# Three stores of a prologue moved to ScalarE's queue, a batch's keys asked for later, the attention pools opened one slot earlier

## Chip, core and metric

One NeuronCore of one Trainium2 chip runs the whole kernel in one launch. The metric is the device time of one execution in microseconds. All data are float32.

## The reference, cut

Four residual layers on x of 64 batches x 32 rows x 512 columns:

```python
x = x + einsum('bct,bcd->bdt', x, L0_weights[cond])            # 32x32 mix of the rows of a batch
x = x + x @ base_weight.T + base_bias + (x @ A[ids].T) @ B[ids].T   # linear layer with a rank 16 adapter
x = x + attention(x)                                           # below
x = x + einsum('bct,bcd->bdt', x, L3_weights[cond])
# attention: q, k, v = x @ Wq.T, x @ Wk.T, x @ Wv.T   (32 query heads, 8 key heads, D = 128)
#   q, k: RMS norm over D, weight, rotary turn by cache_seqlens + row
#   keys, values: 512 rows gathered by pages of 32 from a cache, then the batch's own 32 rows
#   scores masked where the cache row is not below cache_seqlens; softmax; @ values; @ Wo.T
```

## The kernel before, in words

The 2048 rows are 16 tiles of 128 rows (`NT`), four batches to a tile. Attention runs in two halves of the key heads (`NG` = 2), so there are 32 steps of one tile and one half, 128 units of one batch each, and four slots to a unit, one for each key head: slots 0 to 511. Projections are made for two tiles at a time (a *pair*) one pair ahead of the attention that uses them. The slots from -42 to -1 are a prologue: the first two layers (class `First`, tile by tile, two slots apart), the turning of the cache's keys into `kT_dram` (class `Turn`) and the projections of pair 0.

The order of the work is written out by hand. `at(slot, where, do, ...)` puts a call into a plan; `slot(i)` runs the places of slot i in a fixed order: fetch, pool, scores of the slot, values and turns of older slots, then out, pe, take, late, power, turn, dve, keep, act, store. Every engine executes its own instructions in that order and waits for what each needs. A semaphore wait ahead of an instruction holds up everything behind it on the same engine. DMAs started by SP, POOL and ScalarE stand in those engines' streams in the same way.

What the change touches lies between slots -9 and 4:

- Tile 15, the last of `First`, has its turned rows copied out of PSUM by ScalarE (`keep_out`, L497, tile `x_b`) in slot -6, its two sums made by VectorE (`sums`, L507 to L511, tiles `x_12` and `x_34`) in slot -5. `store` (L524) sends the rows to `xT_dram` in slot -5, and `store_sums` (L528) the sums to `xS_dram` in slot -4. For the last three tiles `queue()` gives POOL's queue, for the others SP's.
- In slot -2 the pool `first`, which holds all of the prologue's tiles, is closed, and the pools `pages`, `v`, `attn` and `ps_o` are opened; their tiles may take its memory. A new tile there waits until the old tiles have been read for the last time, by DMAs too.
- In slot -2 POOL also makes the first unit's mask `pen` (`mask`, L819) and starts the gathers of its values (`fetch_values`, L105, tile `v_sb`), two in each of slots -2 and -1. Between them stand the `power` calls of the norms (L725 and L727, tiles `ss` and `rstd`), which turn sums of squares that ScalarE made (L720) into factors that VectorE applies (L732, then L739, L751, L761: the rotary turn).
- In slot 0, `scores` runs two matmuls (L848, L851) into `s_ps`; VectorE adds `pen` and finds the row's top (L856); ScalarE takes the exponentials (L867). There is one `s_ps`, so the next slot's scores wait for L856.
- SP fetches a unit's 16 key pages (`Unit.__init__`, L804, tile `kT`, two buffers): unit 0 in slot -8, unit 1 in slot -1, each later unit in the first slot of the unit before it. SP also loads the next pair's operands: `x_a`, `x_12`, `x_34`, `x_b` (L590) in slots -10, -7, -1, 0 and the rotary factors `rot_k` (L595) in slot 1. L706 stores new values (`vn`) from slot 1 on.

## Time and profile before

| | |
|---|---|
| median of 3 runs | 2436.03 us (2434.91 to 2437.69) |
| the profiled execution | 2439.1 us |
| its span, first to last instruction | 2437.3 us |
| granted TensorE clock | 0.999 |
| TensorE busy | 2401.4 us, 99% of the span |
| VectorE, ScalarE, POOL busy | 68%, 57%, 51% |
| DMA | 452.09 MB, mean 185 GB/s |
| TensorE's share of the chain that ended last | 94% |

Times in the profile are microseconds from the start of the span. Engines are PE (TensorE), PEld (its weight loads), DVE (VectorE), ACT (ScalarE), POOL (GpSimd) and SP; a q behind the name is the queue's own instructions, such as starting a DMA. A timeline row reads: start, length, engine, line and operation, output<-input, count, and in brackets the idle time ahead of it with what ended it. A row of waits reads: who waited, for whom, us in total, times, the longest. A row by stretch reads: stretch, length, then busy time and instructions of PE, PEld, DVE, ACT, POOL, the granted clock, the DMA engines' busy share and GB/s.

### The profile page before, as it was taken

Reading aid. Unit: us, or ns where it says so; the run is one execution under the profiler, and the core shown is the slowest. Engines: PE = TensorE matmul, PEld = TensorE weight load, DVE = VectorE, ACT = ScalarE, POOL = GpSimd, SP = SyncE. Lnnn points to the kernel's source line nnn. Section 1 sums busy time; section 2 is a strip of 40 time slices with the busy share of each in tenths; the row PEclk is TensorE's granted clock in tenths of the full one; section 3 lists DMA queues with packets and bytes.
Section 4 is the critical chain, followed back from the end, with each engine's and each line's share of the span. In section 5 each row is a group of like instructions: output and inputs, shape, how many; then the busy total and the mean of one; then the engine's idle time right before and its main releaser. Section 6 shows DMA issues by size and latency. Waiting matters only on the chain.

```text
span 2437.3 us, 47128 instructions
## 1 busy us (share of the span) xinstructions
PE 2401.4 (99%) x13794; PEld 1865.4 (77%) x13794; DVE 1647.1 (68%) x3554; ACT 1400.6 (57%) x4006; POOL 1234.5 (51%) x1271
## 2 busy tenths in 40 slices
PE   8999999999999999999999999999999999999999
PEld 5657777777777777777777777777777788888887
DVE  6557777777777777787777777777787756333222
ACT  2346777777777777777777777767677763000000
POOL 3336665566565657665665666565556663000000
PEclk9999999999999999999999999999999999999999
DMA  8876667676766677766566666666667874333221
GB/s 275 257 235 188 199 188 204 186 206 184 203 184 203 190 214 241 231 188 194 175 184 176 191 176 184 181 187 182 179 184 225 254 244 144 107 119 122 87 91 58
DMA packets 461199, 452.09 MB, mean 185 GB/s; under 512 B 67744, under 2 KB 384032, under 8 KB 457360
## 3 DMA queue, kind: packets, MB, share of 16 engines
q1 hardware_dynamic: 405104, 269.05, 36.7%
q0 software_dynamic: 55024, 179.25, 25.0%
q8 instruction: 111, 1.82, 0.3%
q14 instruction: 144, 1.18, 0.2%
q10 hardware_dynamic: 816, 0.79, 0.1%
HBM read 380.73 MB, written 76.55 MB: 188 GB/s over the span
## 4 chain that ended last, share of the span: by engine, by line
PE 94%; DMA 2%; DVE 1%; SPq 1%; ACT 1%; issue 1%; POOL 0%; ACTq 0%; DVEq 0%; POOLq 0%
PE proj_ps L664 23%; PE o_ps L900 18%; PE out_ps L1370 15%; PE s_ps L848 10%; PE pT_ps L890 9%; PE s_ps L851 9%; PE head_ps L766 3%; PE l_ps L481 2%; PE o_ps L913 1%; DMA kT<-kT 1%; SPq L804 1%; PE s_ps L883 1%; PE x1T_ps L450 1%; PE proj_ps L1179 1%; DMA o<-oT 1%
## 5 line engine op out<-in xcount | busy, mean ns | idle before, releaser
L105 POOL DMA_INDIRECT v_sb<-v,v_rows x512 | 543.3, 1061 | 361.6 <-PE o_ps L900 248.3
L900 PE MATMUL o_ps<-pT,v_sb 128*128 128x128 f32 x4096 | 624.9, 275 | 3.3 <-DVE pT L892 3.1
L900 PEld LDWEIGHTS o_ps<-pT,v_sb 128*128 128x128 f32 x4096 | 578.0, 191 | 32.2 <-DVE pT L892 5.4
L867 ACT ACTIVATE sm<-sm,top 128x544 f32<-128x544 f32 x512 | 380.8, 744 | 332.8 <-DVE top L856 241.5
L856 DVE CUSTOM_DVE_ANT_0 sm<-s_ps,pen 128x544 f32<-128x544 f32 x512 | 368.9, 721 | 115.4 <-PE s_ps L851 100.0
L873 ACT ACTIVATE sm<-sm,share 128x512 f32<-128x512 f32 x512 | 369.8, 722 | 108.6 <-DVE share L872 71.0
L892 DVE COPY pT<-pT_ps 128x512 f32<-128x512 f32 x512 | 352.9, 689 | 65.5 <-PE pT_ps L890 16.4
L848 PE MATMUL s_ps<-kT,qT 128*128 128x288 f32 x1024 | 334.7, 409 | 4.5 <-DVE top L856 2.7
L890 PE MATMUL pT_ps<-ident,sm 128*128 128x128 f32 x2048 | 310.0, 274 | 4.8 <-ACT qT L778 3.4
L676 DVE TENSOR_TENSOR raw<-proj_ps,raw 128x512 f32<-128x512 f32 x332 | 224.1, 687 | 131.2 <-PE proj_ps L664 118.8
L851 PE MATMUL s_ps<-kT,qT 128*128 128x256 f32 x1024 | 304.7, 379 | 1.3 <-issue 0.7
L848 PEld LDWEIGHTS s_ps<-kT,qT 128*128 128x128 f32 x1024 | 179.2, 190 | 152.4 <-issue 129.9
L819 POOL TENSOR_SCALAR pen<-key_f,seq_f 128x544 f32<-128x544 f32 x128 | 283.7, 2216 | 13.5 <-DMA kT<-kT 2.2
L890 PEld LDWEIGHTS pT_ps<-ident,sm 128*128 128x128 f32 x2048 | 239.3, 142 | 8.7 <-ACT qT L778 4.6
L720 ACT ACTIVATE sq<-raw 128x128 f32<-128x128 f32 x640 | 198.4, 310 | 73.2 <-DVE raw L676 54.6
L851 PEld LDWEIGHTS s_ps<-kT,qT 128*128 128x128 f32 x1024 | 194.4, 190 | 55.7 <-ACT sm L867 1.1
L105 POOL DMA_INDIRECT mix_rows<-in_w,cond_rows x32 | 37.1, 1160 | 343.7 <-DVE mix_diag L170 299.8
L872 DVE RECIPROCAL share<-total 128x1 f32<-128x1 f32 x512 | 83.8, 164 | 179.1 <-ACT sm L867 150.7
L725 POOL TENSOR_SCALAR ss<-ss 128x4 f32<-128x4 f32 x160 | 38.4, 240 | 311.0 <-ACT sq L720 305.1
L1424 ACT COPY p<-out_ps 128x256 f32<-128x256 f32 x7 | 2.6, 372 | 333.1 <-PE out_ps L1370 333.1
L664 PE MATMUL proj_ps<-sum,x 128*128 128x512 f32 x380 | 188.0, 597 | 0.0
L727 POOL TENSOR_TENSOR rstd<-ss,minus_half 128x4 f32<-128x4 f32 x160 | 169.5, 1059 | 13.3
(178 smaller groups left out, 3572.4 us busy)
## 6 DMA issues: line engine op xcount, KB each, us to landing
kT<-kT SPq DMA_DIRECT2D x2048, 64.0 KB
o_in<-o SPq DMA_DIRECT2D x28, 1024.0 KB
o<-oT POOLq DMA_DIRECT2D x68, 256.0 KB
o<-oT SPq DMA_DIRECT2D x58, 256.0 KB
v<-in_kv_cache SPq DMA_DIRECT2D x32, 256.0 KB
kT<-page_rows SPq DMA_DIRECT2D x32, 256.0 KB
vn<-raw SPq DMA_DIRECT2D x32, 256.0 KB
v_sb<-v,v_rows POOLq DMA_INDIRECT x512
```

The source lines that it names most:

```text
L105: nc.gpsimd.indirect_dma_start(out=dst, out_offset=None, in_=table, in_offset=bass.IndirectOffsetOnAxis(ap=index, axis=0),)
L664: nc.tensor.matmul(self.ps, lhsT=self.pair.x[x][:, c if x == "b" else half.start + c, :], rhs=blocks(self.b)[w][:, c, :], start=(c == 0), ...
L819: nc.gpsimd.tensor_scalar(self.pen, key_f, seq_f[:, self.b : self.b + 1], BIG, ALU.is_ge, ALU.mult)
L848: nc.tensor.matmul(ps[:, first:HID], lhsT=q, rhs=self.kT[:, :n1, k, :], start=True, stop=True)
L851: nc.tensor.matmul(ps[:, HID : first + LA], lhsT=q, rhs=self.kT[:, n1:, k, :], start=True, stop=True)
L856: nc.vector.tensor_tensor_reduce(out=sm, in0=ps[:, first : first + LA], in1=self.pen, scale=1.0, scalar=3e38, op0=ALU.add, op1=ALU.min, ac ...
L867: nc.scalar.activation(sm, sm, AF.Exp, bias=top, scale=-1.0, accum_out=total)
L873: nc.scalar.activation(sm[:, :L], sm[:, :L], AF.Copy, scale=share)
L890: nc.tensor.transpose(ps[:, c, :], self.sm[k][:, c * P : (c + 1) * P], ident)
L892: nc.vector.tensor_copy(pT, ps)
L900: nc.tensor.matmul(o_of[self.s, k][:, self.j, :], lhsT=self.v[c][:, k * D : (k + 1) * D], rhs=self.pT[k][:, c, :], start=(self.j == 0 and ...
L1370: nc.tensor.matmul(ps[:, :HALF], lhsT=o[:, i, :], rhs=w[i // REP][:, i % REP, :], start=(i == 0), stop=(i == KG * REP - 1),)
```

## The change

The last tile's `store` moves from POOL in slot -5 to ScalarE in slot -6 (place keep); its `store_sums` from POOL in slot -4 to ScalarE in slot -5 (place turn). Its `store_x` stays on POOL. Unit 1's key pages are asked for in slot 1 instead of -1, so behind `x_34`, `x_b` and `rot_k`. The pool `first` is closed, the attention pools are opened, and the first mask and gathers are made in slot -3 (and two gathers in -2) instead of -2 (and -1).

```diff
-            def queue(self):
-                return nc.sync if self.t < NT - 3 else nc.gpsimd
+            def queue(self, last=nc.gpsimd):
+                return nc.sync if self.t < NT - 3 else nc.gpsimd if self.t < NT - 1 else last
...
             def store(self):
-                self.queue().dma_start(out=xT_dram[self.t], in_=self.x2T)
+                self.queue(nc.scalar).dma_start(out=xT_dram[self.t], in_=self.x2T)
             def store_sums(self):
                 for i in (0, 1):
-                    self.queue().dma_start(out=xS_dram[self.t // 2][:, i], in_=self.s[i])
+                    self.queue(nc.scalar).dma_start(out=xS_dram[self.t // 2][:, i], in_=self.s[i])
...
-            at(home + 4, "store", call, *f, "store")
+            at(*((home + 4, "store") if t < NT - 1 else (home + 3, "keep")), call, *f, "store")
             if t % 2:
                 at(home + 4, "power", call, *f, "sums")
-                at(home + 5, "store", call, *f, "store_sums")
+                where = (home + 5, "store") if t < NT - 1 else (home + 4, "turn")
+                at(*where, call, *f, "store_sums")
...
-            at(KG * (u - 1) if u > 1 else (ready, -1)[u], "fetch", make, unit_of, u, Unit, u)
-            at(KG * (u - 1) + 1 if u else -2, "pool", call, unit_of, u, "mask")
+            at(KG * (u - 1) if u > 1 else (ready, 1)[u], "fetch", make, unit_of, u, Unit, u)
+            at(KG * (u - 1) + 1 if u else -3, "pool", call, unit_of, u, "mask")
             for c in range(NC):
-                at(KG * u - 2 + c if u else -2 + c // 2, "pool", call, unit_of, u, "fetch_values")
+                at(KG * u - 2 + c if u else -3 + c // 2, "pool", call, unit_of, u, "fetch_values")
...
-                if i == -2:
+                if i == -3:
                     first.close()
```

## The prediction

> **What bounds the kernel now.** I read four things in this order: the page (busy shares and the 40 slices), the busy time by stretch, the list of waits between 165 and 190 us, and the timeline of each engine there. TensorE is busy for 99% of the span and holds 94% of the chain that ended last, so a change off TensorE counts only where TensorE stands still. By stretch, that is at one place early on:

> ```profile
> 160.00:170.00 10.00, 9.72 (x36) 4.99 (x34) 6.90 (x14) 4.21 (x14) 1.60 (x4) 1.00 0.63 198
> 170.00:180.00 10.00, 5.69 (x19) 2.78 (x18) 5.58 (x11) 6.15 (x21) 7.21 (x8) 1.00 0.58 179
> 180.00:190.00 10.00, 8.05 (x38) 5.14 (x37) 8.35 (x22) 6.07 (x15) 8.54 (x8) 1.00 0.81 236
> 190.00:200.00 10.00, 10.00 (x58) 7.68 (x57) 5.88 (x14) 5.91 (x16) 6.52 (x9) 1.00 0.72 206
> ```

> The first number after the length is TensorE's busy time. From 170 to 190 us it lacks 4.31 + 1.95 = 6.3 us; before and after it is full, and the granted clock is 1.00 throughout. This is where the attention loop starts (slot 0), and the change edits just this place. The waits name the chain:

> ```profile
> DVE sm L856 <- POOL pen L819: 2.9, 1, 2.9
> ...
> PE s_ps L848 <- DVE top L856: 2.7, 1, 2.7
> POOL pen L819 <- DMA kT<-kT: 2.2, 1, 2.2
> ...
> PEld o_ps L900 <- DMA v_sb<-v,v_rows: 0.3, 1, 0.3
> ```

> TensorE's second scores wait for the first softmax on VectorE, that waits for the mask `pen` on POOL, and that waits for a DMA. Which DMA is seen on POOL's own timeline and in its semaphore waits ahead of L819:

> ```profile
> 169.70 1.05 POOL L727 TENSOR_TENSOR rstd<-ss,minus_half 128x4 f32<-128x4 f32 x1
> 170.72 0.63 POOL L524 DMA_DIRECT2D xT<-x_b  x1
> 171.35 1.08 POOL L528 DMA_DIRECT2D xS<-x  x2
> 172.51 0.48 POOL L725 TENSOR_SCALAR ss<-ss 128x4 f32<-128x4 f32 x1
> 173.07 1.07 POOL L727 TENSOR_TENSOR rstd<-ss,minus_half 128x4 f32<-128x4 f32 x1
> 176.33 2.12 POOL L819 TENSOR_SCALAR pen<-key_f,seq_f 128x544 f32<-128x544 f32 x1 [2.19 <-DMA kT<-kT]
> 178.73 1.11 POOL L105 DMA_INDIRECT v_sb<-v,v_rows  x1 [0.28 <-DMA kT<-kT]
> 180.14 0.96 POOL L105 DMA_INDIRECT v_sb<-v,v_rows  x1 [0.30 <-issue]
> 181.18 0.58 POOL L725 TENSOR_SCALAR ss<-ss 128x4 f32<-128x4 f32 x1
> 181.84 1.04 POOL L727 TENSOR_TENSOR rstd<-ss,minus_half 128x4 f32<-128x4 f32 x1
> ```
> ```profile
> L819 POOLq EVENT_SEMAPHORE  x8: 43/43/2567, 173.0 to 176.2; - x8
> ```

> The long one of the eight waits (2.567 us) is the third, 173.2 to 175.77. In the trace's record of semaphore increments that is the moment at which the second `xS` store of the last tile lands (issued 171.90, so 3.84 us); the name "kT" in the row is only the last DMA that the view found. `pen` takes memory of the pool `first`, which that store still reads. From the landing to `pen` it is 0.56 us.

> **Part 1: the three stores go to ScalarE.** POOL loses 0.63 + 1.08 us of issuing. ScalarE copies `x_b` from 166.21 to 166.80, issues `xT` behind it, then has the head copy (L778, 0.58) and four squares, which end at 169.30 now, and then issues the two `xS`; the sums that they store are ready at 168.39 (L511, 167.97 + 0.42). Rows of a DMA issued by ScalarE and of the same stores from SP:

> ```profile
> L255 ACTq DMA_DIRECT2D page_rows<-in_kv_cache x3: 420/477/1169, 11.8 to 12.8; - x3
> ```
> ```profile
> 129.60 0.89 SPq L528 DMA_DIRECT2D xS<-x  x2
> 130.59 0.45 SPq L521 DMA_DIRECT2D x<-x_sb  x1
> ...
> 134.40 0.33 SPq L398 DMA_DIRECT2D x_sb<-in_x  x1
> ```

> At 0.45 us each, `xT` delays ScalarE by 0.2 (it had a pause of 0.32 there), the squares end near 169.5, and the `xS` are issued at 169.55 and 170.03 instead of 171.35 and 171.90. In the built program the DMAs of SP and ScalarE take eight completion semaphores in turn, and each waits for the one before it on its semaphore; so ScalarE must first see the 10th, 12th and 13th key page of batch 0 land. They do at 166.1, 167.2 and 168.7 in the record of increments, before each is wanted: cost nothing, with 0.7 us of cover at the least. The landing: the pair on SP above took 3.56 and 3.58 us in the increments' record, and the `x` store behind it 3.74; POOL's took 3.84. I take 3.5 (the DMA share is a little lower here without the key pages), bounds 3.0 and 4.6 (the store at 138.44, landed 143.06). So the second `xS` lands at 170.03 + 3.5 = 173.5 and `pen` could start at 173.5 + 0.56 = **174.1 (bounds 173.6 and 175.2)**, 2.2 us earlier than now. ScalarE's eight later squares, the kT copy (173.31), the `raw` copy (173.50) come 1.1 to 1.2 us later, so TensorE's block at 175.55 does too; it is covered by TensorE's pause until 179.27, which has 2.7 us.

> [...]

> **Part 2: the mask and the gathers at slot -3.** This is the part that decides, and it costs. In the built order of the changed kernel POOL has `rstd` (the one of 169.70), then `pen`, two gathers, and only then the pair L725/L727 that now runs at 172.51. VectorE's order is unchanged: its L732 that needs this `rstd` stands ahead of the first softmax.

> ```profile
> 174.17 0.69 DVE L732 TENSOR_TENSOR raw<-raw,rstd 128x512 f32<-128x512 f32 x1 [0.21 <-POOL rstd L727]
> 174.90 0.69 DVE L739 TENSOR_TENSOR rot_a<-raw,rot_q 128x512 f32<-128x512 f32 x1
> 178.48 0.72 DVE L856 CUSTOM_DVE_ANT_0 sm<-s_ps,pen 128x544 f32<-128x544 f32 x1 [2.89 <-POOL pen L819]
> ```
> ```profile
> 179.27 0.75 PE L848 MATMUL s_ps<-kT,qT 128*128 128x288 f32 x2 [2.70 <-DVE top L856]
> ```

> So the `rstd` now waits for the store's landing, the mask and two gathers. From the start of `pen` to the end of an `rstd` behind it today's rows give 182.88 - 176.33 = 6.55 us (with 0.24 instead of 0.58 for L725: 6.2); I take 6.4. `rstd` ends at 174.1 + 6.4 = 180.5. L732 follows at once, L739 0.73 later, the softmax 0.60 to 0.69 after that: 180.5 + 1.4 = **181.9 against 178.48, so +3.4 us** on VectorE, and TensorE's second scores move from 179.27 to 182.7. What follows to 185 us (L751, L761, head turn, pT) hangs on the softmax, one behind another, and moves with it.

> What comes back: the third and fourth gather, now at 183.08 and 184.46, go at about 180.8 and 182.2, so TensorE's wait for the fourth (0.3 us, last line of the waits) goes: **-0.3**. The third `rstd` ends near 184.9 and is wanted 3.4 us later than today's 183.30, at 186.7: hidden, with 1.8 us of cover.

> **Part 3: batch 1's keys behind the pair's operands.** SP now issues `x_34`, `x_b`, two `rot_k` first: `x_34` at about 168.8, `x_b` when TensorE's last matmul on the old one is through (170.4), then the sixteen pages from about 172.9, 10.8 us as now, to 183.7; landing by 186 (1.7 to 3.7 us a page today). Three of these pages wait for the semaphores of ScalarE's stores, free by 173.5. They are wanted by the fifth scores, 190.55 today and 193.6 then: 7 us of cover, nothing on the path. `x_34` and `x_b` are wanted at 196 us or later. The vn store behind them waits for VectorE at 184.60 as it does today. Price **0**; if it reached TensorE, the delay would show as a wait of L848 on kT.

> **The sum.** +3.4 - 0.3 = **+3.1 us**. From 190 us on TensorE has no pause of this kind (all its waits from 190 to 2050 us add to under 13 us), so nothing gives it back. The profiled execution of 2439.1 us (span 2437.3) would be 2442.2 and the span 2440.4; its time is 3.1 us above the median of 2436.03, so I carry the difference to the median: **2439.1**. Per us of landing the sum moves by one us: delta = start of `pen` - 171.0. The bounds 173.6 and 175.2 with 6.2 and 6.55 give +2.4 and +4.4. A measurement of this kernel tells about 0.2%, 4.9 us, from no change.

> **The rivals.**
> - *Slower by more (0.12).* ScalarE's queue is the new bound of the store: an issue of 1.17 us (the longest of the ACTq row) for each instead of 0.45 puts the second `xS` at 171.7, and a landing of 4.6 us puts `pen` at 176.9: delta +5.9, **2441.9**. It decides 0.2% from a `pen` start of 175.9 on. For it: the only three such issues in the trace have one of 1.17. Against: the DMA share is 0.58 at 170 to 180.
> - *The mask leads (0.07).* The softmax follows `pen` and not `rstd`: -2.2 us, **2433.8**. For it: the wait that the view names. Against: in-order VectorE has L732 in front.
> - *It does not do what it says (0.07).* If key pages released `pen`, as the row is named, it would start at 170.8 at once, `rstd` would end at 177.2 and the softmax start at 178.6: no change, **2436**. Against: the 2.567 us wait ends with `xS`.

> **How the numbers follow.** The forecast has 0.74. Its bounds with the spread of the three runs (about 1.4 us either way) are 2437.0 to 2441.8; reaching a little towards the third rival gives 2436.4 to 2441.8, and leaves out the second rival and part of the first. Slower by over 0.2%: the first rival and 0.02 of the forecast's tail, 0.14; faster by over 0.2% needs 4.9 us, which none of these gives, 0.02; the rest 0.84.

> **What would show it.** Right: `pen` at about 174, the L725/L727 pair behind two gathers ending near 180.5, L732 waiting for it, first L856 near 182, TensorE's pause ahead of the second L848 near 6 us. Wrong: L856 before 178.5, a pause on kT at the fifth scores, or a ScalarE issue over 1 us.

## The result, and the profile after

| | before | after | ratio |
|---|---|---|---|
| median, 10 runs each | 2436.16 us | 2441.32 us | 1.0022 (95%: 1.0012 to 1.0031) |
| profiled execution (span) | 2439.1 us (2437.3) | 2437.26 us (2435.5) | |

The changed kernel is slower by about 5 us, with an interval of 3 to 7.5. The two spans say the opposite, because the profiled execution of after is the fastest of its ten and that of before is among its slower ones. What differs between those two for that reason lies near 1980 us and is shown at the end of this section. So the stretch that the change edits has to be compared by itself.

By stretch (start and end, length, busy time and instructions of PE, PEld, DVE, ACT, POOL, granted clock, DMA share, GB/s), after:

```profile
170.00:180.00 10.00, 4.67 (x15) 2.16 (x14) 3.35 (x6) 5.46 (x20) 6.01 (x6) 1.00 0.66 193
180.00:190.00 10.00, 7.84 (x22) 5.14 (x23) 7.56 (x19) 4.86 (x11) 8.57 (x10) 0.66 0.56 165
```

TensorE lacks 5.33 + 2.16 = 7.5 us of work here, 1.2 more than before. The granted clock of 0.66 in the second line is new, so part of the busy time is the same work done at a lower speed. The waits from 165 to 195 us name the new chain:

```profile
DVE raw L732 <- POOL rstd L727: 6.4, 1, 6.4
PE s_ps L848 <- DVE top L856: 5.9, 1, 5.9
...
POOL pen L819 <- DMA rot_k<-trig_all: 3.2, 1, 3.2
```

VectorE's wait for `pen` (2.9 us before) is no longer there. A wait of L732 for `rstd` stands in its place, more than twice as long. ScalarE's queue shows the two `xS` stores, and POOL's timeline shows why `rstd` is late:

```profile
168.75 0.34 ACTq L528 DMA_DIRECT2D xS<-x  x1
...
169.19 0.39 ACTq L528 DMA_DIRECT2D xS<-x  x1
```
```profile
169.50 1.05 POOL L727 TENSOR_TENSOR rstd<-ss,minus_half 128x4 f32<-128x4 f32 x1
173.80 2.12 POOL L819 TENSOR_SCALAR pen<-key_f,seq_f 128x544 f32<-128x544 f32 x1 [3.25 <-DMA rot_k<-trig_all]
176.20 1.11 POOL L105 DMA_INDIRECT v_sb<-v,v_rows  x1 [0.28 <-DMA kT<-kT]
177.62 0.96 POOL L105 DMA_INDIRECT v_sb<-v,v_rows  x1 [0.30 <-issue]
178.65 0.23 POOL L725 TENSOR_SCALAR ss<-ss 128x4 f32<-128x4 f32 x1
178.97 1.05 POOL L727 TENSOR_TENSOR rstd<-ss,minus_half 128x4 f32<-128x4 f32 x1
180.21 1.50 POOL L105 DMA_INDIRECT v_sb<-v,v_rows  x1 [0.20 <-issue]
182.00 0.95 POOL L105 DMA_INDIRECT v_sb<-v,v_rows  x1 [0.30 <-issue]
```

`pen` starts 2.5 us earlier than before (173.80 against 176.33). The pair L725/L727, 1.28 us of work, now stands behind it and two gathers and ends at 180.02; before, it ended at 174.14. The name "rot_k" in the bracket is again only the last DMA that the view found. The semaphore of the second `xS`, issued at 169.19, is full at 173.17 in the record of increments, and `pen` follows 0.63 later. VectorE and TensorE then:

```profile
180.05 0.69 DVE L732 TENSOR_TENSOR raw<-raw,rstd 128x512 f32<-128x512 f32 x1 [6.40 <-POOL rstd L727]
180.77 0.69 DVE L739 TENSOR_TENSOR rot_a<-raw,rot_q 128x512 f32<-128x512 f32 x1
181.38 0.72 DVE L856 CUSTOM_DVE_ANT_0 sm<-s_ps,pen 128x544 f32<-128x544 f32 x1
...
184.48 0.72 DVE L856 CUSTOM_DVE_ANT_0 sm<-s_ps,pen 128x544 f32<-128x544 f32 x1
```
```profile
182.16 1.33 PE L848 MATMUL s_ps<-kT,qT 128*128 128x288 f32 x2 [5.87 <-DVE top L856]
```

The softmax follows L732 and L739 with no wait for `pen`, which had been done since 175.92. TensorE's pause is 5.87 us instead of 2.70. Its first matmul after the pause takes 1.33 us instead of 0.75, because its clock is halved, to 0.50 from 180.79 to 187.61:

```profile
180.00:182.00 2.00, 0.00 (x0) 0.00 (x0) 1.92 (x3) 0.00 (x0) 1.51 (x2) 0.70 0.78 221
182.00:184.00 2.00, 1.84 (x4) 1.47 (x5) 1.06 (x6) 1.63 (x4) 1.84 (x3) 0.50 0.78 231
184.00:186.00 2.00, 2.00 (x4) 0.77 (x4) 1.21 (x3) 0.91 (x3) 1.90 (x2) 0.50 0.50 144
```

Both traces hold the same 13794 matmuls in the same order, so each can be set against its twin. I call the difference lateness, and take its growth from 172 us (ahead of the pause) to 190 us, so that what happened earlier drops out. For after it is **+3.1 us**. By 1900 us it is 0.3 us lower and by 1950 us 1.0 lower, with no step over 0.7.

What turns the two spans round is late. Waits of TensorE from 1945 to 2010 us in before (after has no row of this kind there), then the stretch from 1980 to 2000 us of before and of after:

```profile
PE s_ps L848 <- DMA kT<-kT: 1.6, 1, 1.6
PE s_ps L851 <- DMA kT<-kT: 0.6, 1, 0.6
```
```profile
1980.00:2000.00 20.00, 17.21 (x97) 14.49 (x97) 13.34 (x28) 10.21 (x25) 11.20 (x8) 0.91 0.78 249
```
```profile
1980.00:2000.00 20.00, 18.16 (x114) 15.64 (x115) 13.91 (x28) 10.73 (x26) 10.28 (x9) 1.00 0.75 246
```

In before's profiled execution, key pages come late there and the clock drops. Between 1952 and 2035 us the nine other profiles of this case change their lateness against it by anything from -5.5 to +0.8 us. That is as much as the runs of one kernel scatter (some 4 us either way), so a profile's span can't be used for an effect of 3 us.

### The profile page after: what moved, and what is told of

Its sections match the earlier page's. It is cut to its first block, busy times and chain, and to the rows that moved or that the text cites. A ratio compares the mean times of both kernels' runs of the same rounds, so it can differ in the third digit from the quotient of the medians.

```text
span 2435.5 us, 47125 instructions
## 1 busy us (share of the span) xinstructions
PE 2401.8 (99%) x13794; PEld 1865.5 (77%) x13794; DVE 1650.0 (68%) x3554; ACT 1401.0 (58%) x4006; POOL 1235.3 (51%) x1268
## 3 DMA queue, kind: packets, MB, share of 16 engines
q8 instruction: 111, 1.82, 0.3%
## 4 chain that ended last, share of the span: by engine, by line
PE 95%; DVE 1%; issue 1%; DMA 1%; ACT 1%; POOL 1%; SPq 0%; DVEq 0%; ACTq 0%; POOLq 0%
PE proj_ps L664 23%; PE o_ps L900 18%; PE out_ps L1371 15%; PE s_ps L848 10%; PE pT_ps L890 9%; PE s_ps L851 9%; PE head_ps L766 3%; PE l_ps L481 3%; PE o_ps L913 1%; PE s_ps L883 1%; PE x1T_ps L450 1%; PE h_ps L465 1%; PE mix_ps L1389 1%; PE proj_ps L1180 1%; PE pageT_ps L273 0%
## 5 line engine op out<-in xcount | busy, mean ns | idle before, releaser
L105 POOL DMA_INDIRECT v_sb<-v,v_rows x512 | 545.6, 1066 | 360.4 <-PE o_ps L900 251.7
L900 PE MATMUL o_ps<-pT,v_sb 128*128 128x128 f32 x4096 | 623.9, 275 | 1.7 <-DVE pT L892 1.7
L900 PEld LDWEIGHTS o_ps<-pT,v_sb 128*128 128x128 f32 x4096 | 577.4, 191 | 29.9 <-DVE pT L892 3.0
L856 DVE CUSTOM_DVE_ANT_0 sm<-s_ps,pen 128x544 f32<-128x544 f32 x512 | 369.3, 721 | 110.3 <-PE s_ps L851 97.5
L848 PE MATMUL s_ps<-kT,qT 128*128 128x288 f32 x1024 | 335.4, 409 | 6.3 <-DVE top L856 6.1
L890 PE MATMUL pT_ps<-ident,sm 128*128 128x128 f32 x2048 | 309.6, 274 | 2.3 <-ACT qT L778 2.2
L848 PEld LDWEIGHTS s_ps<-kT,qT 128*128 128x128 f32 x1024 | 179.4, 191 | 154.0 <-issue 129.2
L819 POOL TENSOR_SCALAR pen<-key_f,seq_f 128x544 f32<-128x544 f32 x128 | 283.7, 2216 | 14.6 <-DMA rot_k<-trig_all 3.2
L890 PEld LDWEIGHTS pT_ps<-ident,sm 128*128 128x128 f32 x2048 | 239.0, 142 | 5.9 <-ACT qT L778 3.2
L105 POOL DMA_INDIRECT mix_rows<-in_w,cond_rows x32 | 36.4, 1136 | 345.1 <-DVE mix_diag L170 301.2
L725 POOL TENSOR_SCALAR ss<-ss 128x4 f32<-128x4 f32 x160 | 38.6, 241 | 309.3 <-ACT sq L720 304.1
L727 POOL TENSOR_TENSOR rstd<-ss,minus_half 128x4 f32<-128x4 f32 x160 | 170.1, 1063 | 13.4
```

The costliest lines, as they stand in the source:

```text
L105: nc.gpsimd.indirect_dma_start(out=dst, out_offset=None, in_=table, in_offset=bass.IndirectOffsetOnAxis(ap=index, axis=0),)
L819: nc.gpsimd.tensor_scalar(self.pen, key_f, seq_f[:, self.b : self.b + 1], BIG, ALU.is_ge, ALU.mult)
L848: nc.tensor.matmul(ps[:, first:HID], lhsT=q, rhs=self.kT[:, :n1, k, :], start=True, stop=True)
L856: nc.vector.tensor_tensor_reduce(out=sm, in0=ps[:, first : first + LA], in1=self.pen, scale=1.0, scalar=3e38, op0=ALU.add, op1=ALU.min, ac ...
L890: nc.tensor.transpose(ps[:, c, :], self.sm[k][:, c * P : (c + 1) * P], ident)
L900: nc.tensor.matmul(o_of[self.s, k][:, self.j, :], lhsT=self.v[c][:, k * D : (k + 1) * D], rhs=self.pT[k][:, c, :], start=(self.j == 0 and ...
```

## The experiments

Diffs are against after unless they say otherwise. Each time is a median of 11 runs beside 33 of the kernel before (after's row is the result above, 10 beside 10): before was 2437.56 us for the first four kernels and 2436.46 for the other four. The table gathers what the traces show at the start of attention: when the mask `pen` and the first softmax (L856) start, and how long TensorE pauses ahead of its second scores (PE pause). "Half clock" is the length of the record of the granted clock at 0.5 there. "Late" is the growth of lateness as defined above.

| kernel | median us | ratio (95%) | `pen` | first L856 | PE pause | half clock us | late us |
|---|---|---|---|---|---|---|---|
| before | | 1 | 176.33 | 178.48 | 2.70 | 0 | 0 |
| after | 2441.32 | 1.0022 (1.0012 to 1.0031) | 173.80 | 181.38 | 5.87 | 6.83 | +3.1 |
| e1_again | 2439.25 | 1.0008 (0.9999 to 1.0017) | 173.55 | 181.15 | 5.62 | 6.83 | +2.7 |
| e2_stores_keys | 2434.78 | 0.9985 (0.9976 to 0.9994) | 175.06 | 177.22 | 1.55 | 0 | -0.8 |
| e3_slot3_only | 2441.86 | 1.0023 (1.0013 to 1.0032) | 177.13 | 184.68 | 8.25 | 10.24 | +5.2 |
| e4_no_gather_ahead | 2439.23 | 1.0006 (0.9995 to 1.0017) | 174.73 | 179.65 | 4.50 | 3.41 | +1.5 |
| e5_behind_rstd | 2437.70 | 1.0007 (0.9998 to 1.0016) | 173.57 | 176.28 | 0.73 | 3.41 | +0.6 |
| e6_stores_only | 2436.92 | 1.0000 (0.9991 to 1.0009) | 175.44 | 178.09 | 1.44 | 0 | -0.5 |
| e7_keys_only | 2438.47 | 1.0010 (1.0001 to 1.0019) | 176.78 | 178.94 | 3.06 | 6.83 | +0.6 |
| e8_stores_keys_2 | 2433.17 | 0.9990 (0.9981 to 0.9999) | 174.42 | 177.05 | 0.81 | 0 | -2.2 |

### The changed kernel again (e1_again)

No edit: it shows how far one measurement of the same kernel stands from the next.

> The changed kernel once more. If the loss is all at the start of attention (the rstd behind the mask and two gathers), TensorE is 3 us late at 200 us, no more at the end apart from scatter, and the median is about +3.1 us. If something else in the rest of the span costs too, it is about +5 us and the lateness grows after 200 us. The first softmax (L856) starts near 181.4, TensorE's pause ahead of the second L848 is near 5.9 us and the granted clock halves behind it.

The start of attention repeats within 0.3 us (`pen` 173.55, first softmax 181.15, pause 5.62), but the ratio is 1.0008 instead of 1.0022. The two intervals just overlap. Their mean, 1.0015, is some +3.7 us. Whether after loses more than the 3 us seen at its start stays within this scatter.

### Without slot -3 (e2_stores_keys and e8_stores_keys_2)

```diff
-            at(KG * (u - 1) + 1 if u else -3, "pool", call, unit_of, u, "mask")
+            at(KG * (u - 1) + 1 if u else -2, "pool", call, unit_of, u, "mask")
-                at(KG * u - 2 + c if u else -3 + c // 2, "pool", call, unit_of, u, "fetch_values")
+                at(KG * u - 2 + c if u else -2 + c // 2, "pool", call, unit_of, u, "fetch_values")
-                if i == -3:
+                if i == -2:
                     first.close()
```

> The stores on ScalarE and the later keys stay; pools, mask and gathers go back to slot -2. Theory (the rstd behind the mask is the whole loss): the rstd is made ahead of the mask again, pen starts near 173.8, the first softmax 2.15 us later at 176.0, TensorE's pause is under 1 us: -2.4 us against the kernel before, 2433.8. Rival (the stores on ScalarE or the later keys cost by themselves): slower than before, +1 us or more.

> The kernel with the stores on ScalarE and the later keys, pools at slot -2, once more: its first profile had a landing that let pen start at 175.1 and a gain of 0.6 us at the start of attention, its median was 3.6 us below the kernel before. If the landing scatters, pen starts at another time here, between 173.5 and 175.5, and the first softmax 2.15 us behind it. Median -1 to -3.6 us.

Rows of POOL and PE in e2, then in e8:

```profile
175.06 2.12 POOL L819 TENSOR_SCALAR pen<-key_f,seq_f 128x544 f32<-128x544 f32 x1 [1.72 <-DMA rot_k<-trig_all]
```
```profile
178.00 0.75 PE L848 MATMUL s_ps<-kT,qT 128*128 128x288 f32 x2 [1.55 <-DVE top L856]
...
188.47 0.49 PE L900 MATMUL o_ps<-pT,v_sb 128*128 128x128 f32 x2 [0.45 <-DMA v_sb<-v,v_rows]
```
```profile
174.42 2.59 POOL L819 TENSOR_SCALAR pen<-key_f,seq_f 128x544 f32<-128x544 f32 x1 [0.51 <-DMA rot_k<-trig_all]
```
```profile
177.84 0.75 PE L848 MATMUL s_ps<-kT,qT 128*128 128x288 f32 x2 [0.81 <-DVE top L856]
```

With the pair L725/L727 ahead of the mask again, the earlier store does bring the softmax forward, and the pause shrinks from 2.70 to 1.55 and 0.81. This is the only version that beats both kernels, twice: by 0.15% and by 0.10%, with both intervals below 1. The loss of after is therefore in the slot -3 part, and the two other parts together gain. The medians' 2.4 to 3.7 us (by the ratios) are more than the 0.8 and 2.2 that the traces show at the start; the rest has no place that I could show. The gather's wait, which slot -3 removes, is back as 0.45 us in e2.

### Slot -3 alone (e3_slot3_only)

Against before:

```diff
-            at(KG * (u - 1) + 1 if u else -2, "pool", call, unit_of, u, "mask")
+            at(KG * (u - 1) + 1 if u else -3, "pool", call, unit_of, u, "mask")
-                at(KG * u - 2 + c if u else -2 + c // 2, "pool", call, unit_of, u, "fetch_values")
+                at(KG * u - 2 + c if u else -3 + c // 2, "pool", call, unit_of, u, "fetch_values")
-                if i == -2:
+                if i == -3:
                     first.close()
```

> Only pools, mask and gathers at slot -3; stores on POOL, keys as before. Theory: pen starts as before near 176.2, the rstd behind it ends 6.2 us later near 182.4, the first softmax starts near 183.8 against 178.5, pause near 8 us: +5 us, 2441. Rival (the mask leads, its slot costs nothing): no change, L856 near 178.4.

```profile
183.34 0.69 DVE L732 TENSOR_TENSOR raw<-raw,rstd 128x512 f32<-128x512 f32 x1 [8.74 <-POOL rstd L727]
```
```profile
185.46 1.32 PE L848 MATMUL s_ps<-kT,qT 128*128 128x288 f32 x2 [8.25 <-DVE top L856]
```

With the stores still on POOL, `pen` starts at 177.13 and everything behind it moves with it: `rstd` ends 6.2 us after the start of `pen`, as in after. 1.0023 of 2437.56 is +5.6 us, near the lateness of +5.2. At the start of attention slot -3 alone costs more than the whole change (+5.2 against +3.1 and +2.7; the ratios, 1.0023 against 1.0022 and 1.0008, don't part them as clearly). The stores on ScalarE, with the later keys, take part of it back by letting `pen` start earlier.

### Only the mask ahead (e4_no_gather_ahead)

```diff
-                at(KG * u - 2 + c if u else -3 + c // 2, "pool", call, unit_of, u, "fetch_values")
+                at(KG * u - 2 + c if u else -2 + c // 2, "pool", call, unit_of, u, "fetch_values")
```

> As the changed kernel, but the gathers back in their old slots, so that only the mask stands ahead of the rstd. Theory: pen near 173.8, the rstd ends 3.6 us later at 177.4, the first softmax starts near 178.8 and TensorE's pause is near 3.3 us, without a halved clock: +0.4 us. Rival (the wait for the store's landing is what costs, not what stands between mask and rstd): as the changed kernel, +3 us or more.

```profile
174.73 2.12 POOL L819 TENSOR_SCALAR pen<-key_f,seq_f 128x544 f32<-128x544 f32 x1 [4.52 <-DMA kT<-kT]
176.93 0.23 POOL L725 TENSOR_SCALAR ss<-ss 128x4 f32<-128x4 f32 x1
177.25 1.04 POOL L727 TENSOR_TENSOR rstd<-ss,minus_half 128x4 f32<-128x4 f32 x1
```
```profile
180.43 1.33 PE L848 MATMUL s_ps<-kT,qT 128*128 128x288 f32 x2 [4.50 <-DVE top L856]
```

The store landed later in this execution (5.24 us after its issue at 168.87), so `pen` is 0.9 later than in after. Mainly for that the expectation was missed: the pause is 4.50 us instead of about 3.3, and the clock is halved for 3.41. Measured from `pen`, `rstd` ends 3.56 us on instead of 6.22. The two gathers account for the difference of 2.66, and the lateness falls from +3.1 to +1.5. It is the queue between the mask and `rstd` that sets the cost, with one part for each instruction in it.

### The same place, behind `rstd` (e5_behind_rstd)

```diff
-            at(KG * (u - 1) + 1 if u else -3, "pool", call, unit_of, u, "mask")
+            at(KG * (u - 1) + 1 if u else -3, "pool" if u else "turn", call, unit_of, u, "mask")
-                at(KG * u - 2 + c if u else -3 + c // 2, "pool", call, unit_of, u, "fetch_values")
+                at(KG * u - 2 + c if u else -3 + c // 2, "turn" if u == 0 and c < 2 else "pool", call, unit_of, u, "fetch_values")
```

> The changed kernel with one difference: within slot -3 the mask and its two gathers stand behind the norm's pair L725/L727 instead of ahead of it; pools still open in slot -3. Theory (the place in POOL's order is the loss, not the slot): the rstd is made near 172 to 173, the first softmax starts 2.15 us after pen, 176 to 177.5 with pen at 173.8 to 175.2, and the median is 1 to 3 us below the kernel before. The third rstd stands behind all four gathers here, so up to 1 us of it may come back at the third softmax. Rival (opening the pools at slot -3 or the moved DMAs cost by themselves): +1 us or more.

```profile
176.28 0.72 DVE L856 CUSTOM_DVE_ANT_0 sm<-s_ps,pen 128x544 f32<-128x544 f32 x1 [0.90 <-DMA kT<-kT]
...
183.00 0.69 DVE L732 TENSOR_TENSOR raw<-raw,rstd 128x512 f32<-128x512 f32 x1 [1.82 <-POOL rstd L727]
```
```profile
184.34 3.43 PE L664 MATMUL proj_ps<-sum,x 128*128 128x512 f32 x4 [1.00 <-DVE raw L676]
```

The slot and the stores are those of after; only the order on POOL differs. The first softmax comes at 176.28, 5.1 us earlier than in after and 2.2 earlier than before, and the pause ahead of the second scores shrinks to 0.73. So the order, and not the earlier opening of the pools, costs after its time. Not all of the gain is kept. Four gathers now stand ahead of the third pair L725/L727, VectorE waits 1.82 us for that one, and TensorE pauses 1.00 us and then has its clock halved once: the four matmuls at 184.34 take 3.43 us, where after's at 188.51 take 1.88. The lateness ends at +0.6 and the ratio at 1.0007, so the expected 1 to 3 us below before are not seen.

### The stores alone (e6_stores_only)

The edits of e2, and:

```diff
-            at(KG * (u - 1) if u > 1 else (ready, 1)[u], "fetch", make, unit_of, u, Unit, u)
+            at(KG * (u - 1) if u > 1 else (ready, -1)[u], "fetch", make, unit_of, u, Unit, u)
```

> Only the three stores on ScalarE; keys asked for at slot -1 and pools at slot -2 as before. Theory: the second xS is issued near 169.2 instead of 171.9 and lands at 173 to 174.5 amid the key pages, pen starts 1 to 2.5 us earlier than before and the first softmax with it: -1 to -2.5 us. Rival (with the key pages around it, ScalarE's store lands no earlier than POOL's): no change.

```profile
170.61 1.37 ACTq L528 DMA_DIRECT2D xS<-x  x2
172.10 0.31 ACT L720 ACTIVATE sq<-raw 128x128 f32<-128x128 f32 x1 [2.52 <-DVE raw L732]
```
```profile
175.44 2.62 POOL L819 TENSOR_SCALAR pen<-key_f,seq_f 128x544 f32<-128x544 f32 x1
```

The `xS` stores are issued almost 2 us later than in after, and ScalarE does no work for 2.5 us around them (169.58 to 172.10). The bracket names VectorE; the semaphores name the cause. In the built program the DMAs of SP and ScalarE take eight completion semaphores in turn (100 to 107 in the traces of before and after; in after the two stores have 101 and 102, wait for them at 168.70 and 169.14 and go at 168.75 and 169.19), and with batch 1's keys asked for early, the turn of the two stores falls behind the load of `x_12` and a key page of batch 1. In the record of increments that load is full at 170.53 and the page at 171.58; the stores go at 170.61 and 171.65. ScalarE's squares behind the stores are late too, the pair L725/L727 follows them (L725 at 173.89, done at 175.35), and `pen` starts only when that pair is done. The second store, which landed at 174.72, would not have let it start sooner: the last of the waits ahead of `pen` ends at 175.30. The stores alone gain nothing: 1.0000.

### The keys alone (e7_keys_only)

Against before:

```diff
-            at(KG * (u - 1) if u > 1 else (ready, -1)[u], "fetch", make, unit_of, u, Unit, u)
+            at(KG * (u - 1) if u > 1 else (ready, 1)[u], "fetch", make, unit_of, u, Unit, u)
```

> Only the later request for batch 1's keys. Theory: POOL's stores land 0 to 0.7 us earlier with fewer transfers beside them, the fifth scores wait for no key page: 0 to -0.7 us. Rival (the pages come too late): a wait of L848 on kT at the fifth scores, +1 us or more.

```profile
176.78 2.12 POOL L819 TENSOR_SCALAR pen<-key_f,seq_f 128x544 f32<-128x544 f32 x1 [2.54 <-DMA kT<-kT]
```
```profile
179.73 1.33 PE L848 MATMUL s_ps<-kT,qT 128*128 128x288 f32 x2 [3.06 <-DVE top L856]
```

This was a miss: slower by 0.10% (0.01 to 0.19), where nothing or a small gain was expected. `pen` starts 0.45 us later than in before (POOL's second `xS` store took 4.19 us to land, against 3.84), the pause of 3.06 us brings 6.83 us of halved clock, and the lateness is +0.6. TensorE has no wait on kT at the fifth scores. The ratio's 2.4 us are 1.8 more than that. In this one profile the lateness grows further, to +2.0 by 1900 us, in steps of at most 0.7 us; other profiles show steps as large or larger there, up and down, so the cause of these 1.8 us is open. Together with e6 and e2 it shows that the two parts need each other: alone they give 1.0000 and 1.0010, together 0.9985 and 0.9990.

## Why the prediction was right

It said +3.1 us, and the lateness is +3.1 at the place it named; the median's +5.2 holds it within its interval, and the repeat gives about +2. In absolute time the median of 2441.32 us lies 2.2 above the forecast of 2439.1, near the upper end of the range (2441.8). The steps in its own order:

| step | forecast | after |
|---|---|---|
| second `xS` issued on ScalarE | 170.03 (0.45 us an issue) | 169.19 (0.39) |
| its landing | 3.5 us (3.0 to 4.6) | 3.98 |
| start of `pen` | 174.1 (173.6 to 175.2) | 173.80 |
| `pen` to the end of `rstd` | 6.4 us (6.2 to 6.55) | 6.22 |
| end of `rstd` | 180.5 | 180.02 |
| first L856 | 181.9, +3.4 | 181.38: +2.9, or +3.2 set against a start that was 0.3 earlier |
| wait for the fourth gather | -0.3 | gone; lateness falls by 0.35 at that group of L900 |
| pause ahead of the second L848 | near 6 us | 5.87 |
| clock | nothing said | 6.83 us at half |

**Part 1.** Two terms were off and nearly cancel, which is luck. The stores were put behind the four squares, but their rows start at 168.75 and 169.19, the first while the last square (168.69, 0.31 us) still runs. ScalarE's queue issued them when their own semaphore waits were met (at 168.70 and 169.14 in the trace), the second 0.84 us earlier than forecast. And the landing took 3.98 us instead of 3.5. That term is the least certain of the sum. For this one store, by its own semaphore, the profiles where it releases `pen` show 3.66 (e5), 3.67 (e1), 3.83 (e8), 3.98 (after), 5.04 (e2) and 5.24 us (e4). The last two are past the upper bound of 4.6, taken from the longest landing of such a store in one profile.

**Part 2** carried the forecast, and its mechanism is shown from four sides: undone in e2 and e8, done alone in e3, the queue behind the mask shortened in e4, only the order reversed in e5.

**Part 3** was priced at 0 with cover for the keys themselves, which held: no wait on kT appears at the fifth scores. What the price left out is what else the pages stood in front of: asked for early, one of them holds a completion semaphore that ScalarE's stores need. Part 1's forecast rested on that too. It was right only because part 3 moves the pages away (in e6, without part 3, the first store goes at 170.61 instead of 168.75), and the prediction read the semaphores of the whole change without asking which part made them free. e7's loss is the other side that a price of 0 didn't foresee.

**The clock** was not thought of, and the sum still holds. The lateness grows to +5.0 us while TensorE runs at half speed, and goes back to +3.4 because two of before's pauses behind that (0.50 us at 181.81 and one ahead of L890) vanish; the gather's wait takes it to +3.1. VectorE sets the pace here. Its second softmax is 2.89 us later than before's (184.48 against 181.59) and its third 3.16 (188.27 against 185.11), so the slow matmuls cost at most 0.3 us more than the pause itself.

**The rivals.** "Slower by more" fell on both its terms: the issues take 0.34 and 0.39 us, and with the stores on ScalarE no landing brought `pen` to the 175.9 that it needed, though 175.06 (e2) and 174.73 (e4) came within 1.2 us. (Its 171.7 also leaves out ScalarE's pause of 0.32 us, which the forecast had deducted; with it the sum gives about 171.4.) "The mask leads" is what e5 does, where the order lets it. The third was wrong: `pen` did move.

## What to carry to other kernels

Before a step is moved earlier on an in-order engine, list what it passes and who waits for that. Here a mask that waits 3 us for a store was put ahead of 1.3 us of work that the same softmax needs first. When a wait is shortened and a step moved in one change, measure the parts apart: here two parts together gain 0.10 to 0.15%, neither does so alone, and the third hides it. And for an effect of one or two thousandths compare instructions with their twins at the place of the edit, not spans.
